# A 7x7 convolution's own steps: another order of reads, scaling and queues

## The chip, the cores and the metric

The kernel runs on one core of a Trainium2 chip. Its time is the device time of one execution in microseconds (us), lower is better. A time of the kernel is the median of several runs; a profiled execution of its own gives the trace.

## The reference

Two residual layers over an input `x` of shape (8, 96, 96, 192) in float32: eight images of 96 x 96 pixels with 192 channels.

```python
# layer 0: group norm, 1x1 projection to 384 channels, 3x3 depthwise convolution,
#          four directional running means, layer norm, 1x1 projection back
x = x + _L0_conv_ref(_gn(x), L0_conv_W_in, L0_conv_b_in, L0_conv_conv_w, ...)
# layer 1
x = x + _L1_conv_ref(_gn(x), L1_conv_dw_kernel, L1_conv_dw_bias, ...)

def _L1_conv_ref(x, dw_kernel, dw_bias, ln_gamma, ln_beta, w0, b0, w1, b1, gamma):
    y = lax.conv_general_dilated(x, dw_kernel, window_strides=(1, 1), padding='SAME',
            dimension_numbers=('NHWC', 'HWIO', 'NHWC'), feature_group_count=c) + dw_bias
    mu = jnp.mean(y, axis=-1, keepdims=True)
    var = jnp.mean(jnp.square(y - mu), axis=-1, keepdims=True)
    y = (y - mu) * lax.rsqrt(var + EPS) * ln_gamma + ln_beta
    y = jnp.einsum('bhwc,cd->bhwd', y, w0) + b0          # 192 -> 768
    y = jax.nn.gelu(y, approximate=False)
    y = jnp.einsum('bhwd,dc->bhwc', y, w1) + b1          # 768 -> 192
    return y * gamma
```

`_gn` is a group norm with 32 groups of 6 channels over a whole image. The depthwise kernel of layer 1 is 7x7, one filter for each channel.

## The kernel before, in words

The kernel has five phases, each with an order of instructions written out by hand (`manual_schedule`): what stands earlier in the code stands earlier in each engine's queue. Phases A to C do layer 0 and leave its result, called x1, in the DRAM tensors `X1_d`, one for each half of the batch (four images). Phase D does the group norm and the 7x7 convolution of layer 1, phase E its layer norm and the two large projections (the "last pass").

**Phase D** runs in steps. `todo` lists 32 of them: for each batch half 16 blocks of 12 channels (two groups of 6). The first `N1` = 19 steps, numbers 0 to 18, run by themselves ("own steps"); the other 13 are fed in small pieces into the first half of phase E. So all of batch half 0 (steps 0 to 15) is convolved before phase E starts. A step n consists of

- `load_raw(n, t)`, t = 0 to 2: x1's rows of the block, each t as two DMAs of 64 partitions (g = 0 and 1). Rows of step n + 2 are loaded during step n, into a buffer that step n's rows leave.
- `load_band(n)`: the convolution's band matrix, one DMA into half of the partitions; a copy on VectorE (`spread` in `scale_steps`) makes the other half.
- `scale_steps(n)`: the group norm as 24 scalings of 128 x 192 elements (8 for each t) from `raw` to `xin`, on VectorE, for steps 1 and 18 (t = 1, 2) and all later ones on ScalarE.
- `conv_d(n, c)`, c = 0 to 5: 12 matmuls into two PSUM banks, and two evictions on ScalarE into `yo` (L1197).
- `store_d(n)`: six DMAs from `yo` to the DRAM tensor `Y_d`, three for each of the block's two groups.

During step n the loop issues, in this order: the first rows of step n + 2, the stores of step n - 1, the rest of the rows and the band of step n + 2, one piece of `norm_c(1)` (the group statistics of batch half 1, from step 3 on), the scalings of step n + 1, and the six convolutions of step n.

DMAs are issued from two engines' queues, SyncE's (SP) and GpSimd's (POOL). The rows of g = 0 and the stores of the first group are SP's, those of g = 1 and of the second group POOL's, and the bands alternate.

**Phase E** works on tiles of `Y_d`. `load_y(n)` reads tile n with 41 pieces: `begin`, which takes the buffers `ya` and `yb`, and 40 DMAs, five for each of eight blocks q of 32 partitions. q = 0 to 5 stand for channel blocks 0 to 5 (each five groups of 6 channels, so that block 0 needs no more than steps 0 to 2, block 4 steps up to 12, block 5 steps up to 14), q = 6 and 7 repeat blocks 4 and 5; the fifth DMA of each q brings a part of the last two groups, which step 15 makes. A tile serves two units u (`per` = 2); there are 72 units. For each unit `norm_steps_e(u)` is the layer norm in seven pieces: `sums`, `mean`, `center` (VectorE), `square` (ScalarE, L1340), `squares`, `powers` (VectorE, and a power on GpSimd, L1352) and `scale` (VectorE). Then `turn_in` transposes on VectorE, `first_layer` projects to 768 channels (L1388, L1398) with a Gelu on ScalarE (L1407), and `second_layer` projects back (L1418), adds the residual `r` (L1429, x1 read by `load_r` and biased by GpSimd, L1269), and stores the output from GpSimd (L1437).

At the end of phase D the two phases overlap: in step 16 (`NI`) the reads of tile 0 are issued between the convolutions, in step 18 those of tile 1; in step 17 the layer norm of unit 0 begins, in step 18 that of unit 1. The scalings of step 18 for t = 1 and 2 are placed on ScalarE three at a time between the evictions of step 17, and the pieces `square` and after it are placed behind its last convolutions:

```python
parts = load_y((n - NI) // 2) if n in (NI, NI + 2) else []
if n >= NI + 1:
    held, chain = chain, norm_steps_e(n - NI - 1)
    for step in chain[:3] + held:
        step()
    chain = chain[3:]
for c in range(GS):
    conv_d(n, c)
    for step in parts[c * 7 : c * 7 + 7]:
        step()
    for step in steps[c * 3 : c * 3 + 3]:
        step()
    if n >= NI + 1 and c >= GS - 3:
        chain.pop(0)()
```

Of the kernel before, what the change touches and what calls it, by code (L numbers as in the profile page):

```python
# [15 lines left out]
GROUPS = 32  # L16
# [85 lines left out]
def conv_blocks_kernel(  # L102
# [716 lines left out]
    def load_raw(n, t):  # L819
# [13 lines left out]
        for g, eng in enumerate((nc.sync, nc.sync if n >= N1 else nc.gpsimd)):  # L833
# [9 lines left out]
    def load_band(n):  # L843
# [5 lines left out]
        (nc.sync, nc.gpsimd)[g and n < N1].dma_start(  # L849
            band[g * 64 : (g + 1) * 64].rearrange("q c l -> q (c l)"),  # L850
            Z2_d[:, i * GC : (i + 1) * GC].rearrange("r c l -> r (c l)"),
        )

    def scale_steps(n):
# [4 lines left out]
        def scale(t, k, b):  # L859
            if (t, k, b) == (0, 0, 0):  # L860
                pool = d_pools[0 if n >= N1 else n % 2]
                xins[n] = pool.tile([128, NT, NH, GC, WV], F32, tag="xin", name="xin")
# [27 lines left out]
    def norm_c(hf, bank):  # L890
# [7 lines left out]
        def means():  # L898
            ms = gp.tile([128, GROUPS], F32, tag="gn_ms", name="gn_ms")
            nc.vector.tensor_reduce(ms, sv[:, :, :, 1], AX.X, ALU.add)  # L900
            t["ps"] = bank()
            nc.tensor.matmul(t["ps"][:, :GROUPS], blk, ms, start=True, stop=True)

        def squares():
            t["gm"] = gm = gp.tile([128, GROUPS], F32, tag="gn_gm", name="gn_gm")
# [12 lines left out]
            ds = gp.tile([128, GROUPS], F32, tag="gn_ds", name="gn_ds")  # L918
            nc.vector.tensor_reduce(ds, d, AX.X, ALU.add)
            t["ps"] = bank()  # L920
            nc.tensor.matmul(t["ps"][:, :GROUPS], blk, ds, start=True, stop=True)

        def powers():
            ve = gp.tile([128, GROUPS], F32, tag="gn_ve", name="gn_ve")
# [21 lines left out]

        def keep():
            nc.vector.tensor_copy(
                s1[:, hf].rearrange("p b a g -> p (b a g)"),
                t["ps"][:, : NH * 2 * GROUPS],  # L950
            )

        return [means, squares, powers, shift, spread, keep]
# [251 lines left out]
    def store_d(n):  # L1205
# [5 lines left out]
        for k, eng in enumerate((nc.sync, nc.sync if n >= N1 else nc.gpsimd)):  # L1211
            y_d = Y_d[hf][:, 2 * i + k].rearrange("r b a n -> r (b a n)")
            eng.dma_start(  # L1213
# [3 lines left out]
            eng.dma_start(y_d[:e], yf[k * 64 : k * 64 + e, 0])  # L1217
            eng.dma_start(y_d[ROWS - e :], yf[k * 64 + KB - e : k * 64 + KB, NB - 1])  # L1218
# [223 lines left out]
    with tc.manual_schedule():  # L1442
        with tc.tile_pool(name="d_own", bufs=1, side="right", **by_tile) as own:
            d_pools[1] = own
            norms, chain = norm_c(1, bank), []
            for n in range(N1):
                if n + 2 < N1:
                    load_raw(n + 2, 0)
                if n:
                    store_d(n - 1)  # L1450
                if n + 2 < N1:
                    for t in range(1, NT):
                        load_raw(n + 2, t)
# [6 lines left out]
                now = len(steps) if n + 2 < N1 else len(steps) // NT  # L1460
# [145 lines left out]
```

## Time and profile before

| | |
|---|---|
| median of 3 runs | 5567.61 us (5566.02 to 5573.98) |
| profiled execution, its own time | 5583.44 us |
| its span, first to last instruction | 5581.6 us |
| PE (matmul) busy | 5300.3 us, 95% |
| DVE, ACT, POOL busy | 65%, 46%, 42% |
| DMA, GpSimd's queue (q0) | 332.38 MB, 18.3% of 16 engines |
| DMA, SyncE's queue (q1) | 673.77 MB, 47.9% of 16 engines |
| convolution, L1187 | 4608 matmuls, 433.2 us busy, 514 ns each |
| evictions, L1197 | 384 on ACT, 198.8 us busy, 579 ns each |
| first layer, L1388 and L1398 | 785.9 and 419.6 us busy |
| second layer, L1418 | 6912 matmuls, 1175.4 us busy |

The profile is of one execution. Engines are PE (TensorE's matmuls), PEld (its weight loads), DVE (VectorE), ACT (ScalarE), POOL (GpSimd) and SP (SyncE). Busy time leaves out issuing and waiting. The idle time ahead of an instruction is put down to what released it; where a wait is for several things, to the one that came last. A share of DMA is the busy share of the core's 16 DMA engines, with both queues together. The mean over the span says little here, since the phases have different limits; the stage of the own steps lies between about 2650 and 3010 us.

### The profile page before, as it was taken

What the parts mean: (1) busy time and instruction counts of PE and PEld (TensorE: products, weight loads), DVE (VectorE), ACT (ScalarE), POOL (GpSimd) and SP (SyncE); (2) the same over time, 40 slices, a digit from 0 to 9 for tenths busy, and PEclk for the clock granted to TensorE, in tenths of its full rate; (3) what the DMA queues carried; (4) which work ended last, traced back from release to release, by engine and by line L of the source; (5) the groups of instructions that cost most, each with busy time, mean ns of one, the idle gap of its engine ahead of it and who ended that gap; (6) DMA issues with size and microseconds to landing.
All of it is one profiled execution on the core that took longest, in us unless ns stands there. A gap on an engine that the chain in (4) does not pass through costs nothing. (4 is left out here: it accounts for less than half of the span.)

```text
span 5581.6 us, 108128 instructions
## 1 busy us (share of the span) xinstructions
PE 5300.3 (95%) x42206; PEld 3355.4 (60%) x42206; DVE 3600.3 (65%) x6722; ACT 2588.8 (46%) x5778; POOL 2320.5 (42%) x2035
## 2 busy tenths in 40 slices
PE   6999989999999999998686999999899999999999
PEld 4666633333333999997343555566566676667667
DVE  6656449999999455555454655555566676776764
ACT  2444447777776556554433444444433233333332
POOL 1111128888887555554222222232233333333332
PEclk9999989999999999999897999999999999999999
DMA  7999879999997899999996554565433332233331
GB/s 221 286 293 264 240 194 243 244 246 241 245 245 205 260 292 287 281 290 275 253 280 157 118 120 108 128 135 135 110 89 92 82 81 77 79 89 90 81 79 40
DMA packets 801788, 1015.29 MB, mean 182 GB/s; under 512 B 331345, under 2 KB 684690, under 8 KB 799229
## 3 DMA queue, kind: packets, MB, share of 16 engines
q1 hardware_dynamic: 713445, 673.77, 47.9%
q0 software_dynamic: 81872, 332.38, 18.3%
q8 instruction: 333, 5.46, 0.4%
q10 hardware_dynamic: 5960, 2.22, 0.2%
q14 instruction: 178, 1.46, 0.1%
HBM read 603.70 MB, written 419.95 MB: 183 GB/s over the span
## 5 line engine op out<-in xcount | busy, mean ns | idle before, releaser
L1418 PEld LDWEIGHTS hp<-w1g,g 128*128 128x128 f32 x6912 | 1118.4, 190 | 141.6 <-issue 73.5
L1418 PE MATMUL hp<-w1g,g 128*128 128x192 f32 x6912 | 1175.4, 329 | 0.0
L1407 ACT ACTIVATE g<-hp,b0g 128x512 f32<-128x512 f32 x864 | 518.3, 690 | 1143.4 <-PE hp L1398 1143.4
L1437 POOL DMA_DIRECT2D out_dram<-xo x288 | 210.6, 731 | 1647.5 <-DVE xo L1429 1561.1
L1388 PE MATMUL hp<-yT,w0w 128*128 128x512 f32 x1728 | 785.9, 601 | 21.8 <-DVE yT L1373 17.6
L1429 DVE TENSOR_TENSOR xo<-hp,r 128x384 f32<-128x384 f32 x288 | 227.5, 790 | 821.6 <-PE hp L1418 812.7
L1026 PE MATMUL po<-wc,mt 128*128 128x193 f32 x3456 | 688.0, 335 | 7.1 <-DVE x1c L1043 6.8
L627 PE MATMUL pl<-pin,band 34*32 34x380 f32 (+1 forms) x13824 | 629.0, 490 | 20.4 <-DMA pin<-P_d 20.4
L701 POOL TENSOR_TENSOR mo<-mo,z 128x768 f32<-128x768 f32 x286 | 597.8, 2090 | 4.4 <-ACT mo L652 0.4
L1026 PEld LDWEIGHTS po<-wc,mt 128*128 128x128 f32 x3456 | 557.6, 192 | 37.8 <-ACT mean L1028 30.4
L1187 PE MATMUL hp<-xin,band 63*64 63x372 f32 (+1 forms) x4608 | 433.2, 514 | 147.0 <-ACT xin L868 50.2
L1388 PEld LDWEIGHTS hp<-yT,w0w 128*128 128x128 f32 x1728 | 324.0, 192 | 387.3 <-issue 349.0
L660 DVE TENSOR_TENSOR_SCAN z<-decay,loc 128x768 f32<-128x768 f32 x288 | 505.5, 1755 | 45.1 <-ACT loc L636 16.7
L669 DVE TENSOR_TENSOR_SCAN z<-decay,z 128x768 f32<-128x768 f32 x288 | 498.3, 1730 | 0.1
L627 PEld LDWEIGHTS pl<-pin,band 34*32 34x32 f32 x13824 | 232.3, 107 | 399.0 <-issue 397.1
L1352 POOL TENSOR_TENSOR rs<-tot,neg_half 32x32 f32<-32x32 f32 x72 | 394.6, 5481 | 94.5 <-DVE tot L1350 94.4
L648 PE MATMUL pa<-loc,mix 128*32 128x384 f32 x3456 | 432.0, 494 | 0.0
L651 PE MATMUL pa<-last,down 96*32 96x384 f32 x1152 | 426.9, 494 | 0.9 <-ACT mo L652 0.9
L1398 PE MATMUL hp<-yT,w0w 64*128 64x512 f32 x1728 | 419.6, 611 | 0.0
L1187 PEld LDWEIGHTS hp<-xin,band 63*64 63x64 f32 x4608 | 212.3, 142 | 337.5 <-issue 187.1
L1197 ACT ACTIVATE yo<-hp,dwb 128x384 f32<-128x384 f32 x384 | 198.8, 579 | 432.2 <-PE hp L1187 308.8
L636 ACT COPY loc<-pl 128x384 f32<-128x384 f32 x576 | 248.1, 483 | 313.1 <-PE pl L627 313.1
(158 smaller groups left out, 7521.6 us busy)
## 6 DMA issues: line engine op xcount, KB each, us to landing
pin<-P_d SPq DMA_DIRECT2D x192, 576.0 KB
P_d<-po POOLq DMA_DIRECT2D x95, 1152.0 KB, 9.7
mt<-M SPq DMA_DIRECT2D x192, 384.0 KB
xq<-in_x_dram SPq DMA_DIRECT2D x96, 576.0 KB
xr<-in_x_dram SPq DMA_DIRECT2D x192, 288.0 KB
X<-x1c SPq DMA_DIRECT2D x144, 384.0 KB
r<-X SPq DMA_DIRECT2D x36, 1536.0 KB
out_dram<-xo POOLq DMA_DIRECT2D x288, 192.0 KB, 2.5
```

What stands on the lines that cost most here:

```text
L627: nc.tensor.matmul(pls[g][at * RB : (at + 1) * RB, :, lo:hi], band[rows, c, kh, :], pin[rows, c, :, NJ - 1 - j, lo + kh - 1 : hi + kh - 1] ...
L648: nc.tensor.matmul(pa[at], mix[:, i, at], loc[:, q], start=True, stop=True)
L651: nc.tensor.matmul(pa[at], down[:, to], last[:, q], start=True, stop=True)
L660: nc.vector.tensor_tensor_scan(zf, decay_f, loc.rearrange("p q n -> p (q n)"), 0.0, ALU.mult, ALU.add)
L669: nc.vector.tensor_tensor_scan(zr, decay_f, zr, 0.0, ALU.mult, ALU.add)
L701: eng.tensor_tensor(m, m, z, ALU.add)
L1026: nc.tensor.matmul(po, lhs[m], wc[:, m], start=(m == 0), stop=(m == NC - 1))
L1187: nc.tensor.matmul(pys[g][k * 64 : (k + 1) * 64, :, lo:hi], band[rows, k * GS + c, d * ZS : d * ZS + 64], xin[rows, :, :, k * GS + c, lo + ...
L1388: nc.tensor.matmul(hps[m, q], w0w[:, 0, m * 128 : (m + 1) * 128], yT[:, 2 * q], start=True, stop=False,)
L1398: nc.tensor.matmul(hps[m, q], w0w[p, 1, m * 128 : (m + 1) * 128], yT[p, 1], start=False, stop=True,)
L1407: nc.scalar.activation(g[:, m, q], hps[m, q], AF.Gelu, bias=b0g[:, m : m + 1], scale=1.0)
L1418: nc.tensor.matmul(po[:, q], g[:, m, q, k * 128 : (k + 1) * 128], w1g[:, m], start=(m == 0), stop=(m == NE - 1),)
```

## The change

Five things change in the own steps.

- Rows: from step 2 to 18 all six row DMAs are issued by GpSimd, ahead of everything else in the step.
- Stores and bands: all are issued by SyncE, in the own steps as later; the band of step n + 2 stands ahead of the stores of step n - 1.
- Tile 0 of the last pass: its reads are issued in steps 12, 13, 14 and 16, as soon as the steps that make their channels have been stored; tile 1's are issued at the end of step 17, ahead of the store of that step.
- The end: in step 17 the band copy and the first three pieces of unit 0's layer norm stand ahead of VectorE's scalings of step 18, and ScalarE's 16 scalings and the `square` stand behind all evictions of step 17. In step 18, unit 0's `squares` and `powers`, unit 1's first three pieces and unit 0's `scale` stand ahead of the convolutions, and unit 1's `square`, `squares` and `powers` behind them.
- `norm_c`: the matmul that sums over partitions is issued with the piece that reads its result, one piece later than before, and `keep` is joined to `spread`.

```diff
@@ load_raw
-        for g, eng in enumerate((nc.sync, nc.sync if n >= N1 else nc.gpsimd)):
+        engs = (nc.sync, nc.gpsimd) if n < 2 else (nc.gpsimd,) * 2 if n < N1 else (nc.sync,) * 2
+        for g, eng in enumerate(engs):
@@ load_band
-        (nc.sync, nc.gpsimd)[g and n < N1].dma_start(
+        nc.sync.dma_start(
@@ norm_c
         def means():
-            ms = gp.tile([128, GROUPS], F32, tag="gn_ms", name="gn_ms")
+            t["in"] = ms = gp.tile([128, GROUPS], F32, tag="gn_ms", name="gn_ms")
             nc.vector.tensor_reduce(ms, sv[:, :, :, 1], AX.X, ALU.add)
+
+        def total():
             t["ps"] = bank()
-            nc.tensor.matmul(t["ps"][:, :GROUPS], blk, ms, start=True, stop=True)
+            nc.tensor.matmul(t["ps"][:, :GROUPS], blk, t["in"], start=True, stop=True)

         def squares():
+            total()
...
-            t["ps"] = bank()
-            nc.tensor.matmul(t["ps"][:, :GROUPS], blk, ds, start=True, stop=True)

         def powers():
+            total()
@@ store_d
-        for k, eng in enumerate((nc.sync, nc.sync if n >= N1 else nc.gpsimd)):
+        for k in range(2):
...
-            eng.dma_start(
+            nc.sync.dma_start(
@@ own steps
-            norms, chain = norm_c(1, bank), []
+            make_xin(1)
+            norms = norm_c(1, bank)
+            y_0, y_1 = load_y(0), load_y(1)
+            early_y = {
+                NI - 4: y_0[:1] + [y_0[1 + q * 5 + b] for q in (0, 1) for b in range(NH)],
+                NI - 3: [y_0[1 + q * 5 + b] for q in (2, 3) for b in range(NH)],
+                NI - 2: [y_0[1 + q * 5 + b] for q in (4, 6) for b in range(NH)],
+                NI: [y_0[1 + q * 5 + b] for q in (5, 7) for b in range(NH)]
+                + [y_0[1 + q * 5 + NH] for q in range(8)],
+                NI + 1: y_1,
+            }
             for n in range(N1):
                 if n + 2 < N1:
-                    load_raw(n + 2, 0)
+                    for t in range(NT):
+                        load_raw(n + 2, t)
+                    if n:
+                        load_band(n + 2)
                 if n:
                     store_d(n - 1)
-                if n + 2 < N1:
-                    for t in range(1, NT):
-                        load_raw(n + 2, t)
+                else:
                     load_band(n + 2)
...
                 steps = scale_steps(n + 1) if n + 1 < N1 else []
-                now = len(steps) if n + 2 < N1 else len(steps) // NT
-                for step in steps[:now] + steps[-1:] * (now < len(steps)):
+                last, on_scalar = [], []
+                if n == NI + 1:
+                    chain = norm_steps_e(0)
+                    per_t = len(steps) // NT
+                    on_scalar = steps[per_t:-1]
+                    steps = steps[-1:] + chain[:3] + steps[:per_t]
+                    on_scalar.insert(per_t, chain[3])
+                    chain = chain[4:]
+                elif n == NI + 2:
+                    nxt = norm_steps_e(1)
+                    steps = chain[:2] + nxt[:3] + chain[2:]
+                    on_scalar = nxt[3:6]
+                    chain = nxt[6:]
+                for step in steps:
                     step()
...
                 for c in range(GS):
                     conv_d(n, c)
-                    for step in parts[c * 7 : c * 7 + 7]:
-                        step()
-                    for step in steps[c * 3 : c * 3 + 3]:
-                        step()
-                    if n >= NI + 1 and c >= GS - 3:
-                        chain.pop(0)()
+                for step in on_scalar + early_y.get(n, []):
+                    step()
```

More of the change, by code (lines that the diff above doesn't have):

```diff
@@ L852, in load_band, with make_xin @@
         )
+    def make_xin(n):
+        pool = d_pools[0 if n >= N1 else n % 2]
+        xins[n] = pool.tile([128, NT, NH, GC, WV], F32, tag="xin", name="xin")
     def scale_steps(n):
@@ L859, in scale @@
         def scale(t, k, b):
-            if (t, k, b) == (0, 0, 0):
-                pool = d_pools[0 if n >= N1 else n % 2]
-                xins[n] = pool.tile([128, NT, NH, GC, WV], F32, tag="xin", name="xin")
+            if n not in xins:
+                make_xin(n)
             c = slice(k * GS, (k + 1) * GS)
@@ L917, in squares @@
             )
-            ds = gp.tile([128, GROUPS], F32, tag="gn_ds", name="gn_ds")
+            t["in"] = ds = gp.tile([128, GROUPS], F32, tag="gn_ds", name="gn_ds")
             nc.vector.tensor_reduce(ds, d, AX.X, ALU.add)
-            t["ps"] = bank()
-            nc.tensor.matmul(t["ps"][:, :GROUPS], blk, ds, start=True, stop=True)
         def powers():
+            total()
             ve = gp.tile([128, GROUPS], F32, tag="gn_ve", name="gn_ve")
@@ L945, in spread @@
                 )
-        def keep():
             nc.vector.tensor_copy(
@@ L951, in keep @@
             )
-        return [means, squares, powers, shift, spread, keep]
+        return [means, squares, powers, shift, spread]
     with ExitStack() as ph:
@@ L1216, in store_d @@
             )
-            eng.dma_start(y_d[:e], yf[k * 64 : k * 64 + e, 0])
-            eng.dma_start(y_d[ROWS - e :], yf[k * 64 + KB - e : k * 64 + KB, NB - 1])
+            nc.sync.dma_start(y_d[:e], yf[k * 64 : k * 64 + e, 0])
+            nc.sync.dma_start(y_d[ROWS - e :], yf[k * 64 + KB - e : k * 64 + KB, NB - 1])
     def place(n):
@@ L1459, in conv_blocks_kernel @@
                 steps = scale_steps(n + 1) if n + 1 < N1 else []
-                now = len(steps) if n + 2 < N1 else len(steps) // NT
-                for step in steps[:now] + steps[-1:] * (now < len(steps)):
-                    step()
-                steps = steps[now:-1]
-                parts = load_y((n - NI) // 2) if n in (NI, NI + 2) else []
-                if n >= NI + 1:
-                    held, chain = chain, norm_steps_e(n - NI - 1)
-                    for step in chain[:3] + held:
-                        step()
-                    chain = chain[3:]
+                last, on_scalar = [], []
[12 more added lines that the diff above has]
+                for step in steps:
+                    step()
                 for c in range(GS):
                     conv_d(n, c)
-                    for step in parts[c * 7 : c * 7 + 7]:
-                        step()
-                    for step in steps[c * 3 : c * 3 + 3]:
-                        step()
-                    if n >= NI + 1 and c >= GS - 3:
-                        chain.pop(0)()
+                for step in on_scalar + early_y.get(n, []):
+                    step()
             store_d(N1 - 1)
```

## The prediction

> **What bounds the kernel now.** I read the page's 40 slices first, to find where PE, which is busy for 95% of the span, has holes.
>
> ```profile
> PE   6999989999999999998686999999899999999999
> DMA  7999879999997899999996554565433332233331
> ```
>
> A slice is 139.5 us. Slices 20 to 22 (2651 to 3070 us) read 6, 8 and 6 for PE, its longest stretch below 9 in the run; here lie the 19 convolution steps. In the first two of them the DMA engines are full, in the third they are not. So it has two limits. The table of stages splits it (times from the span's start, then PE, PEld, DVE, ACT and POOL busy, granted clock, DMA share, GB/s):
>
> ```profile
> core 0: us, PE busy (x) PEld busy (x) DVE busy (x) ACT busy (x) POOL busy (x), PEclk, DMA share, GB/s
> 2684.00:2720.00 36.00, 19.19 (x217) 10.30 (x209) 14.42 (x44) 10.18 (x20) 8.55 (x13) 0.81 1.03 297
> 2720.00:2732.00 12.00, 9.56 (x90) 4.28 (x94) 7.50 (x18) 2.89 (x6) 1.88 (x4) 0.71 0.50 119
> 2732.00:2946.00 214.00, 172.31 (x1872) 98.09 (x1864) 111.17 (x323) 79.24 (x155) 57.43 (x83) 0.91 1.02 282
> 2946.00:3008.00 62.00, 27.16 (x288) 14.53 (x288) 31.89 (x78) 24.18 (x44) 10.60 (x9) 0.74 0.48 116
> 3008.00:3055.00 47.00, 33.50 (x91) 14.64 (x92) 21.71 (x43) 13.62 (x19) 8.71 (x5) 0.76 0.71 160
> ```
>
> Up to 2946 the 16 DMA engines are the limit (share 1.02 to 1.03), but for a hole of 12 us at a share of 0.50. The timeline puts the last eviction (L1197) of step 2 at 2694.5 and that of step 16 at 2945.6: 251.1 / 14 = 17.9 us a step, where neighbouring steps that wait for no data take 11.4. After 2946 neither PE nor DMA is full: there waits decide. The table of waits (total, times, longest) for 2940 to 3060 names them:
>
> ```profile
> DVE s L1325 <- DMA yb<-Y: 39.5, 3, 17.7
> POOL r L1269 <- DMA ya<-Y: 38.3, 1, 38.3
> PE hp L1187 <- ACT xin L868: 27.8, 1, 27.8
> ACT sq L1340 <- DVE ya L1318: 23.1, 1, 23.1
> ```
>
> and the timeline the order (start, duration, engine, line, and in brackets the idle time and who ended it):
>
> ```profile
> 2985.07 1.96 ACT L1340 ACTIVATE sq<-ya 128x1024 f32<-128x1024 f32 x1 [23.11 <-DVE ya L1318]
> 2990.07 13.85 PE L1187 MATMUL hp<-xin,band 63*64 63x384 f32 x144 [27.83 <-ACT xin L868]
> 3008.57 6.32 PE L1388 MATMUL hp<-yT,w0w 128*128 128x512 f32 x8 [4.65 <-DVE yT L1373]
> 3039.68 2.05 PE L1388 MATMUL hp<-yT,w0w 128*128 128x512 f32 x2 [11.78 <-DVE yT L1373]
> ```
>
> Read upwards from PE: step 18 waits 27.8 us for its scaled rows on ACT; ACT stands 23.1 us at the square of the first tile (L1340), placed among the evictions of step 17; the square waits for DVE's centring, and that for the tile's last read from Y. All 41 reads of tile 0 are issued only between 2944.5 and 2978.8. The second tile repeats it: PE stands 11.8 us at 3039.7. From 3100 on PE is 90 to 100% busy, so what is won here reaches the end.
>
> **What the Trainium skill says.** "DMA: Bandwidth & Descriptors", section "Issuing engines are not separate DMA queues": DMAs of all issuing engines run on the same 16 engines and interleave; issuing from several only saves sequencer time. The trace agrees on the sharing: both queues together make up the share of 1.02. Hence moving x1's rows to GpSimd adds no engine. The same page, section "Queues, rings and completion order": each DMA engine goes round robin between the queues it has work for. So splitting rows (one queue) from stores (the other) mixes reads and writes all the time, where before each queue carried a run of stores and then a run of rows. What a mix is worth this trace shows, below. "TensorE: Matmul & The Clock Gate", section "What's actually happening": an idle array falls to half clock. The granted clock of 0.71 to 0.76 in the stretches with holes, against 0.91, agrees; fewer holes give a little more that I don't count.
>
> **The change, part by part.**
>
> *DMA-bound steps.* Rows (L839): 102 issues of 384 KB for steps 2 to 18. Half leave SP for POOL. POOL's issue costs 0.715 us each, 6 a step = 4.3 us; 19 x 3 stores (0.70 + 0.53 + 0.58) and its bands (0.55) leave POOL, so its load is as before and far under a step. POOL's queue loses its 155 us of waits for evictions (L1213), behind which rows stood; rows now wait only for DVE's scaling, which frees their buffers, and for the landing of the row load eight earlier on the queue (so the built program orders it). Behind a waiting row stands one pow of 5.65 us (L928), needed ten steps later: nothing. SP takes 6 stores and one band a step, some 2.5 us of issue; behind its wait for evictions stands only a band for a step later.
>
> The price is DMA time. At equal share the rate differs by what is in flight (windows 2898 to 2903, then 2784 to 2789; q1 is SP's queue, q0 GpSimd's):
>
> ```profile
> DMA packets 675, 1.16 MB, mean 231 GB/s; under 512 B 41, under 2 KB 575, under 8 KB 675
> q1 hardware_dynamic: 664, 1.10, 103.5%
> ```
>
> ```profile
> DMA packets 578, 1.91 MB, mean 383 GB/s; under 512 B 78, under 2 KB 174, under 8 KB 561
> q0 software_dynamic: 298, 1.15, 60.9%
> q1 hardware_dynamic: 280, 0.77, 41.9%
> ```
>
> SP's rows go in packets under 2 KB (575 of 675 here); GpSimd's go in larger ones. Over 2650 to 2946, 79.3 MB move at 268 GB/s: 296 us. Bounds: if only the queue's average counts (q1 39.57 MB in 52.0% of 296 us = 257 GB/s, q0 39.33 MB in 46.0% = 289), 20 MB go over and 19 MB come back, a gain of 0. If the mix is always that of the second window, 79.3 / 0.383 = 207 us, a gain of 89, of which 16 steps at 11.4 us of PE allow no more than about 80. I take 296 GB/s: 6 us from the hole (12 us at half share), which lifts 268 to 274, and a third of the way from there to 340, the middle of two windows rich in GpSimd's packets (297 and 383). 79.3 / 0.296 = 268 us, a gain of 28.
>
> The hole: PE waited 9.6 us for the group sums (L900) and 9.6 us until DVE read the sum out of its bank (L906). The change issues each of these matmuls a step later, just before its reader, so both waits go; in full-DMA time they cost nothing, their worth is the 6 us of the hole, counted above.
>
> *Early reads of tile 0.* 24 of its 40 loads (60 KB each) move into steps 12 to 14, 8 and the 8 small ones to the end of step 16. Each is an SP issue of 0.44 us; 8 in a step are 3.5 us, behind which one band and six stores queue: hidden under 17.9. Their DMA time is not hidden: alone on the queue (2955 to 2978) they make 1.79 MB in 32.2% of 23 us, 240 GB/s; 1.5 MB / 240 = 6 us, lost. Stage: -28 + 6 = **-22 us** (range -70 to +6).
>
> *The tail*, from the start of step 17 (before: 2948.9). DVE: band copy 1.5, sums 1.9 + 1.0, mean 2.7, centring 2.4 = 9.5 us, then 8 scalings, 2.4. ACT: evictions to 12.0; 8 scalings at 0.48 = 3.9; square 2.0 + 1.1, no longer waiting, since centring ends at about 9.5; 8 scalings 3.9: 22.9. PE's step 18 runs 22.9 to 34.3, evictions to 35.1. DVE meanwhile does tile 0's squares and powers and unit 1's sums, mean and centring (both units read tile 0), and pow (5.45 on POOL) lies beside them; scale(0) ends by 34. Then, in order on DVE ahead of the transposes: square of unit 1 on ACT, 3.1 (38.2), squares 1.75 and powers 1.65 (41.6), first transpose 1.0: PE's first L1388 at **42.7**. Before it was 3008.6 - 2948.9 = 59.7: -17. PE's stall of 27.8 becomes one of about 11.5 (17 ACT-side operations now stand ahead of step 18) and the one of 4.7 becomes 8. So "behind evictions" is not free; it is cheaper than the wait.
>
> Then 11.8 us at 3039.7: tile 1's 41 loads, 36 us of issue on SP, now start right after step 16's store, about at 0, and land near 37; first needed after 42.7. -12, with only 6 us of cover: if SP is slower, part returns. Step 17's store and then r's load now stand behind them: issued near 45, landed (15 us as before) and biased (5.4) by 66; first reader L1429 near 74. Tail: **-29 us** (range -42 to -10). The reordered sums of image half 0, in the stage before, are one instruction each: 0 (+-3).
>
> Sum: -22 - 29 = -51. The profiled execution itself took 5583.4 us around a span of 5581.6; the median of the runs is 5567.6. The difference is applied to the median: **5517 us**.
>
> **The rivals.**
> 1. *As above*: 5517, own range 5497 to 5540. Chance 0.50.
> 2. *The DMA engines are full and stay so.* The queue averages (257 against 289, swapped evenly) speak for it; the mixed windows against. Stage +6, or 0 with the hole; tail -26: 5567.6 - 26 + 3 = 5545. Chance 0.20.
> 3. *The mix pays fully*: 340 GB/s, 79.3 / 0.340 = 233, stage -57, tail -29: 5482. For it: 383 and 314 GB/s in windows with stores. Chance 0.15.
> 4. *Tail gives its gain on*: tile 1's reads or r come late and PE stands at 3039's place again: tail -10, stage 0: 5558. Chance 0.04.
> 5. *Slower: x1's rows on one queue become the bound.* Six loads a step, at most eight in flight: a step can't be under 6/8 of a load's landing. The median landing is 13.6 us now (10.2 us a step, harmless), with three rows a step and the stores on that queue. Were it 30 us, a step would take 22.5: 15 x 4.6 = +69, less 29: 5608. It decides from where the 29 are eaten, a step of 17.9 + 29/15 = 19.8 us, a landing of 26.5. Against it: POOL's rows take half of the bytes today within the same landing as stores. Chance 0.11.
>
> **How the numbers follow.** A change under 0.2% (11 us) can't be told from none by a measurement of this kernel. Rivals 1, 2 and 3 are faster: 0.85; rival 4 straddles the limit: same 0.04; rival 5 slower: 0.11. The range leaves out most of rival 5 and the far half of rival 3: 5478 to 5562.
>
> **What would show it.** Right: from step 2 to step 16 a step takes 16 us rather than 17.9; no share of 0.50 near 2725; PE's wait on ACT xin (L868's successor) near 11 us; first L1388 near 43 us after step 17's first matmul; no 11.8 us wait at unit 1. Wrong: DVE's scaling waits longer for raw than 107.6 us in the stage, or POOL's rows land after 20 us and more (rival 5); the rate stays at 268 GB/s (rival 2); sums (L1325) still wait for yb (rival 4).

## The result, and the profile after

The changed kernel takes 5545.5 us, the median of 8 runs (5537.57 to 5560.37), beside 5572.44 us (5564.01 to 5581.5) of the kernel before on the same chip: a ratio of 0.9955, 95% interval 0.9941 to 0.997. So it is faster by 27 us (17 to 33), about half of the 51 us forecast.

Two profiled executions of one kernel differ: the phases before the own steps end anywhere between 2620 and 2652 us in the executions shown here, whatever the kernel. So totals are compared by their medians, and stages by their own length. Three lengths are used throughout, read from the timelines: **own steps**, from the last projection matmul of phase C to step 16's last eviction; **12 to 16**, the part of it between the last evictions of steps 12 and 16; **tail**, from step 16's last eviction to the first Gelu of unit 3.

| kernel | own steps | 12 to 16 | tail |
|---|---|---|---|
| before, first and second profile | 313.0, 300.9 | 67.7, 62.4 | 179.9, 181.8 |
| after, first and second profile | 299.0, 304.7 | 78.0, 76.0 | 156.0, 159.3 |

The own steps have hardly gained, 302 us against 307 in the mean; the tail has, 158 against 181. First the page's 40 slices of the kernel after, as they were read for the kernel before:

```profile
PE   6999989999999999999786999999999999999999
DMA  7999879999997899899996555555433233333331
```

The low stretch is still three slices, 7, 8 and 6 where it was 6, 8 and 6. The table of stages of the kernel after (from and to; busy time of PE, PEld, DVE, ACT and POOL; granted clock, DMA share, GB/s):

```profile
2684.00:2720.00 36.00, 28.98 (x317) 16.97 (x309) 22.14 (x61) 12.26 (x25) 9.96 (x14) 0.91 1.02 327
2720.00:2732.00 12.00, 11.76 (x138) 6.77 (x142) 9.21 (x29) 5.49 (x12) 8.57 (x5) 1.00 1.02 344
2690.00:2860.00 170.00, 148.67 (x1654) 91.43 (x1658) 103.22 (x293) 69.47 (x140) 54.68 (x68) 0.93 1.01 316
2860.00:2935.00 75.00, 50.23 (x557) 35.85 (x552) 27.60 (x76) 23.70 (x48) 8.23 (x13) 0.82 0.88 230
```

Up to 2860 the step has changed as meant: the DMA engines are as full as before, but move 316 GB/s, where the two profiles of before have 274 and 280 in the same stretch (2690 to 2860); the second profile of after has 307. The hole with a share of 0.50 is gone, and a step takes 15.1 us. From 2860 to 2935, in steps 13 to 16, it turns round: 230 GB/s at a share of 0.88, PE busy for only 50 of 75 us, 19.5 us a step. The table of waits from 2640 to 2950 (total, times, longest) shows what is new there:

```profile
POOL raw L840 <- DVE xin L874: 163.5, 40, 24.3
ACT yo L1201 <- DMA Y<-yo: 103.5, 13, 14.9
...
PE hp L1191 <- ACT yo L1201: 69.4, 13, 19.4
...
ACT yo L1201 <- DMA ya<-Y: 27.9, 2, 21.6
```

The last line puts 21.6 us of one eviction's wait (L1201) down to a *read* of tile 0, with which an eviction has nothing to do. What it needs is its output buffer, and so the landing of an older store; but DMAs raise a few semaphores in turn when they land (experiment 2), and the profile takes the wrong one for the releaser. That reads are behind it all the same, the timeline of the kernel after tells (start, duration, engine, line; SPq is SyncE issuing):

```profile
2842.32 14.45 SPq L1250 DMA_DIRECT2D ya<-Y  x8
2856.88 1.33 SPq L850 DMA_DIRECT2D band<-Z_d  x1
2858.32 0.54 SPq L1217 DMA_DIRECT2D Y<-yo  x1
...
2869.33 0.26 SPq L1222 DMA_DIRECT2D Y<-yo  x1
2869.68 15.06 SPq L1250 DMA_DIRECT2D ya<-Y  x8
2884.29 3.88 ACT L1201 ACTIVATE yo<-hp,dwb 128x384 f32<-128x384 f32 x8 [21.61 <-DMA ya<-Y]
2884.86 0.45 SPq L850 DMA_DIRECT2D band<-Z_d  x1
2885.41 0.54 SPq L1217 DMA_DIRECT2D Y<-yo  x1
```

Eight reads take SyncE 14.5 and 15.1 us, not 3.5. Step 12's stores go out from 2858.3 to 2869.3, 8 us and more after its last eviction at 2850.2; step 13's only from 2885.4. There are two output buffers in turn, so step 14's evictions stand until step 12's stores have landed (the last, issued at 2869.3, lands at 2884.1), and PE stands behind them.

The tail, in the timeline of the kernel after (idle time ahead and who ended it in brackets):

```profile
2935.71 1.90 DVE L1329 TENSOR_REDUCE s<-ya 128x32 f32<-128x1024 f32 x1 [11.71 <-DMA yb<-Y]
...
2942.90 1.97 ACT L1344 ACTIVATE sq<-ya 128x1024 f32<-128x1024 f32 x1
2948.75 13.57 PE L1191 MATMUL hp<-xin,band 63*64 63x384 f32 x144 [10.35 <-ACT xin L872]
2970.66 6.51 PE L1392 MATMUL hp<-yT,w0w 128*128 128x512 f32 x8 [8.33 <-DVE yT L1377]
2990.11 3.70 PE L1392 MATMUL hp<-yT,w0w 128*128 128x512 f32 x8
2997.42 0.55 SPq L1267 DMA_DIRECT2D r<-X  x1
3013.56 5.43 POOL L1273 TENSOR_TENSOR r<-r,b1g 128x3072 f32<-128x3072 f32 x1 [38.50 <-DMA ya<-Y]
3019.02 0.79 DVE L1433 TENSOR_TENSOR xo<-hp,r 128x384 f32<-128x384 f32 x1 [23.84 <-DMA ya<-Y]
3032.36 6.77 PE L1422 MATMUL hp<-w1g,g 128*128 128x192 f32 x24 [7.81 <-DVE xo L1433]
```

The square waits for nothing, PE stands 10.4 us ahead of step 18 instead of 27.8 and 8.3 ahead of the first layer, and the 11.8 us ahead of unit 1 are gone. The sums of unit 0 (L1329) do still wait 11.7 us for the last reads of tile 0, which the prediction names as a sign of being wrong. It costs little: the centring of `ya` ends at 2942.5, 0.4 us before ScalarE comes to its square. Then VectorE waits 23.8 us at the first output (L1433) until r is biased at 3019.0 (the brackets name a read here, too, though it is r that is missing). PE's stops that follow, here and 4.1 us at 3019.9, give back 13 us: counted from step 16's last eviction, unit 1's first Gelu comes 36.9 us earlier than in the first profile of before, unit 2's only 23.9.

### The profile page after: what moved, and what is told of

It is laid out like the page before. It is cut to its first block, busy times and chain, and to the rows that moved or that the text cites. A ratio compares the mean times of both kernels' runs of the same rounds, so it can differ in the third digit from the quotient of the medians.

```text
span 5535.8 us, 108053 instructions
## 1 busy us (share of the span) xinstructions
PE 5289.6 (96%) x42206; PEld 3367.3 (61%) x42206; DVE 3595.9 (65%) x6722; ACT 2588.6 (47%) x5778; POOL 2319.7 (42%) x2020
## 2 busy tenths in 40 slices
DMA packets 795469, 1015.27 MB, mean 183 GB/s; under 512 B 330623, under 2 KB 671728, under 8 KB 792912
## 5 line engine op out<-in xcount | busy, mean ns | idle before, releaser
L1392 PE MATMUL hp<-yT,w0w 128*128 128x512 f32 x1728 | 780.9, 598 | 14.9 <-DVE yT L1377 8.3
L1433 DVE TENSOR_TENSOR xo<-hp,r 128x384 f32<-128x384 f32 x288 | 227.4, 790 | 834.4 <-PE hp L1422 810.4
L1392 PEld LDWEIGHTS hp<-yT,w0w 128*128 128x128 f32 x1728 | 321.8, 191 | 377.7 <-issue 339.2
L660 DVE TENSOR_TENSOR_SCAN z<-decay,loc 128x768 f32<-128x768 f32 x288 | 505.5, 1755 | 45.8 <-ACT loc L636 17.3
L1191 PEld LDWEIGHTS hp<-xin,band 63*64 63x64 f32 x4608 | 224.8, 140 | 294.4 <-issue 125.9
L382 PE MATMUL pm<-xT,win 128*128 128x384 f32 x1152 | 392.7, 491 | 0.0
```

Of the source, the lines that this page charges most:

```text
L660: nc.vector.tensor_tensor_scan(zf, decay_f, loc.rearrange("p q n -> p (q n)"), 0.0, ALU.mult, ALU.add)
L1191: nc.tensor.matmul(pys[g][k * 64 : (k + 1) * 64, :, lo:hi], band[rows, k * GS + c, d * ZS : d * ZS + 64], xin[rows, :, :, k * GS + c, lo + ...
L1392: nc.tensor.matmul(hps[m, q], w0w[:, 0, m * 128 : (m + 1) * 128], yT[:, 2 * q], start=True, stop=False,)
```

## Experiments

All lengths are from one profile of each kernel, all ratios against the kernel before from five rounds of runs; "early reads" are the 24 reads of tile 0 in steps 12 to 14. The edits are shown shortened.

**1. What does each part do? (four kernels)** The change once more; the queue part alone on the kernel before; the change without early reads; the change with r's load moved forward.

> The changed kernel once more, with a second profile, beside the others of this set. The pair of profiles at hand differs by 45.8 us of span, the medians of eight runs by 27. If the 45.8 is the luck of two executions, this profile gives a difference nearer 27 and its stretch from step 2's last eviction to step 16's will differ from the first profile's 229 us by several us. If the pair is typical, the ratio here is 0.992 or lower.

The queue part alone takes the kernel before, changes `load_raw`, `load_band`, `store_d` and the order of rows, band and stores as the change does, and leaves reads, scalings and `norm_c`:

> The kernel before with only the queue part: from step 2 on all rows from GpSimd, stores and bands from SyncE, in the changed order. Reads of tiles 0 and 1, scalings, layer norm and the group sums as before. My theory (rows in one queue and stores in the other mix better): steps 2 to 16 at 15 us instead of 17.9, DMA at 315 to 325 GB/s, and with a tail as before some 32 us less than before: ratio 0.994. The rival (the DMA engines were full and stay so; the gain of the change comes from its tail): 17.5 us or more a step, ratio 0.999 to 1.000.

No early reads:

```diff
-    NI - 4: ..., NI - 3: ..., NI - 2: ..., NI: ...,
+    NI: y_0,
     NI + 1: y_1,
```

> The changed kernel, but all 41 reads of tile 0 are issued at the end of step 16, none in steps 12 to 14. My theory: the early reads stop SyncE for 14 to 15 us each time, stores and bands behind them come late, and steps 12 to 16 pay 10 to 17 us for it. So here step 12 to step 16 takes 60 us (15 a step) instead of 78, while the first tile now lands some 36 us after step 16 and step 18 starts about 26 us later: in sum 5 to 12 us slower than the changed kernel. The rival (the early reads are hidden, other things delay steps 12 to 16): step 12 to 16 stays near 78 us, and the sum is 26 us or more slower than the changed kernel.

And r first:

```diff
-            store_d(N1 - 1)
-            load_band(N1)
-            for t in range(NT - 1):
-                load_raw(N1, t)
         gn_pool.close()
...
         load_r(0)
+        store_d(N1 - 1)
+        load_band(N1)
+        for t in range(NT - 1):
+            load_raw(N1, t)
```

> The changed kernel, with the residual's first load ahead of step 18's stores and of step 19's band and rows on SyncE, instead of behind them. My theory: in the changed kernel the second wait of the tail is not gone but moved to the residual, whose first reader stands 23.8 us and PE about 14 us for it; here the residual lands 8 to 13 us earlier and the kernel is 8 to 13 us faster than the changed one (ratio to before about 0.993 to 0.994). The rival (the residual is not on the path, PE has other work): same as the changed kernel within 3 us.

| kernel | median us | ratio, 95% | own steps | 12 to 16 | tail |
|---|---|---|---|---|---|
| the change again | 5546.97 | 0.9952 (0.9936 to 0.9968) | 304.7 | 76.0 | 159.3 |
| queue part alone | 5528.41 | 0.9929 (0.9911 to 0.9947) | 278.4 | 54.4 | 173.2 |
| no early reads | 5537.89 | 0.9939 (0.9923 to 0.9955) | 275.0 | 53.8 | 173.5 |
| r first | 5529.46 | 0.9925 (0.9909 to 0.9941) | 301.9 | 81.3 | 147.1 |

The change's second profile is 36.1 us of span under before's first, not 45.8, so a part of that difference was chance. The queue part alone wins at least as much as the whole change, and as its theory said: 14.7 us a step from 2 to 16. Its two windows, steps 2 to 12 and 12 to 16 (columns as above):

```profile
2690.00:2845.00 155.00, 134.64 (x1523) 77.16 (x1519) 96.23 (x274) 61.38 (x122) 50.07 (x61) 0.94 1.02 321
2845.00:2899.00 54.00, 48.82 (x577) 36.49 (x573) 34.57 (x100) 23.64 (x48) 13.37 (x19) 0.97 0.99 320
```

320 GB/s all the way. It also fills the hole near 2725 (share 1.02 from 2720 to 2732, and PE waits no more than 0.4 us for the group sums), though it leaves `norm_c` as it was. So the early reads take some 25 us from the own steps and give the tail 14 to 17; its theory also said that the kernel without them would be 5 to 12 us slower in sum. Its median is 9 us lower, and the two intervals overlap: that is not borne out. And r was worth 9 to 12 us of the tail, as expected, but it is soon followed by the next two late things, in the timeline of "r first":

```profile
3021.05 0.80 DVE L1433 TENSOR_TENSOR xo<-hp,r 128x384 f32<-128x384 f32 x1 [6.03 <-POOL r L1273]
...
3061.25 1.02 DVE L1329 TENSOR_REDUCE s<-yb 128x16 f32<-128x512 f32 x1 [14.33 <-DMA yb<-Y]
...
3074.58 3.77 PE L1191 MATMUL hp<-xin,band 63*64 63x384 f32 x24 [9.36 <-DVE band L878]
```

VectorE's wait for r falls from 23.8 to 6.0 us, but step 19's band, which r overtook, now stops PE for 9.4.

**2. Why do the early reads cost 25 us? (three kernels)** Their DMA time, counted as 6 us in the forecast; the order in SyncE's queue; or something in the reads themselves. First two ways round SyncE's queue: fewer reads in a step, or another engine.

```diff
-    NI - 4: 8 reads, NI - 3: 8 reads, NI - 2: 8 reads
+    steps 5 to 8 and 11 to 15: 2 to 4 reads each
```

> The change, but tile 0's early reads two to four a step over steps 5 to 8 and 11 to 15 instead of eight in each of steps 12 to 14; the rest at the end of step 16 as in the change. Theory (SyncE's queue): a DMA waits for the landing of the one eight earlier on its queue, so a step can't be shorter than its DMAs on that queue / 8 x their landing: 15 / 8 x about 10.4 us = 19.5 us in steps 12 to 14 of the change. With 9 to 11 a step it is about 13 us, under the 13.6 us that a step takes with no early reads: step 12 to 16 falls from 76-78 us to about 57, the tail stays as in the change; about 5525 us. Rival (the reads' own DMA time): the same bytes are moved in the same full stage, nothing changes: about 5545 us.

With r's load forward as well:

> The spread reads, and r's load issued ahead of step 18's stores and of step 19's band and rows. Theory: both losses are separate, so the sum of both gains: some 20 us in the steps and 10 in the tail, about 5513 us. Rival (the reads' own DMA time is the loss in the steps): only r's part, about 5532 us. Rival (r's wait is given on to step 19's band and rows): as the spread reads alone.

```diff
 def piece(q, b, eng=nc.sync):
...
+    step(nc.scalar)     # the early reads; the others as before
```

> The change, but the 24 early reads of steps 12 to 14 are issued by ScalarE on a queue of its own, at the same place, behind the step's evictions. Bytes, packets and moments stay. Theory (SyncE's queue): SyncE is back to 7 DMAs a step, its stores go out at once; step 12 to 16 falls to about 58 us, less whatever ScalarE's issue of 8 x 0.44 us delays evictions; about 5527 us. Rival (DMA time, or many small packets): nothing changes, step 12 to 16 stays at 76 us, about 5545 us.

| kernel | median us | ratio, 95% | own steps | 12 to 16 | tail |
|---|---|---|---|---|---|
| spread | 5552.34 | 0.9968 (0.9956 to 0.998) | 304.0 | 71.5 | 160.9 |
| spread, r first | 5538.94 | 0.9943 (0.9926 to 0.996) | 294.1 | 67.4 | 152.7 |
| from ScalarE | 5547.58 | 0.9959 (0.9944 to 0.9973) | 298.5 | 72.5 | 159.7 |

All three miss what the theory expected. SyncE's own waits tell why. First those of the change (2840 to 2935):

```profile
SPq L1250 <- DMA Y<-yo: 18.3, 6, 4.9
SPq L1250 <- DMA band<-Z_d: 5.4, 2, 3.2
SPq L1222 <- DMA ya<-Y: 5.2, 2, 3.6
```

Reads (L1250) wait for the landing of stores and of a band, stores (L1222) for that of reads. It is not for their data: in the traces each DMA raises a semaphore when it lands, SyncE's and ScalarE's DMAs take eight such semaphores in turn, GpSimd's eight others, and a read that waits here waits for the semaphore that it will raise itself, that is for the DMA eight earlier. So the second of step 12's reads is issued at 2845.8, when the band that was issued at 2829.5 has landed. From ScalarE (2855 to 2935):

```profile
SPq L1222 <- DMA Y<-yo: 22.7, 3, 8.9
SPq L1221 <- DMA ya<-Y: 14.6, 4, 6.7
```

SyncE's stores (L1221) wait for reads that *ScalarE* issued, and no data passes between the two; the eight semaphores are common to both. So the move to ScalarE did not take the reads off the stores' way, and ScalarE, which was held for 11 us by the first eight reads, kept its own evictions waiting besides. Spread (2738 to 2935):

```profile
SPq L1250 <- DMA band<-Z_d: 26.0, 7, 6.1
SPq L850 <- DMA Y<-yo: 18.9, 7, 5.0
```

With 9 to 11 DMAs in a step the eighth earlier one is still of the same step: reads wait for the band and the stores just issued, and the next band waits in turn. My formula in the expectation (DMAs / 8 x landing) gave 13 us a step and no loss; it averages over a step, and the queue doesn't (a reading of these waits; no run tests it).

**3. The reads' packets, or their number? (three kernels)** The same reads in unbroken stretches:

```diff
-    y[:, chunk * main : (chunk + 1) * main, b, a]                       # 5 x 384 bytes a row
+    y[:, chunk * main + b].rearrange("r b a n -> r (b a n)")[:, :480]   # 1920 bytes a row
```

> The change, but each of the 24 early reads of steps 12 to 14 takes one unbroken stretch of 1920 bytes from each of its 32 rows, where it takes five pieces of 384 bytes; same place in SyncE's queue, same bytes, same step dependences (so tile 0 gets wrong channels). Theory of packets ([...]160 packets of 384 bytes wait for as many packets of rows and bands, and the queue behind the read waits too): with 32 packets a read is issued and done at once; step 12 to 16 falls from 76-78 us to 56-60, the total by some 18 us to about 5527. Rival (a read stands behind stores and the band because the queue takes no more than eight DMAs at a time): the packets don't matter, SyncE still has 15 DMAs in a step, step 12 to 16 stays above 70 us, about 5543 us.

Then four such reads in one DMA, six instead of 24 (the first of the two kernels also issued joined reads for all later tiles, so only its own steps can be read):

> The change, but the 24 early reads of 60 KB are joined into six of 240 KB, two in each of steps 12 to 14, of unbroken stretches of 1920 bytes as in the run before (so tile 0 gets wrong channels). Bytes and packets are those of that run, only the number of DMAs falls. Theory (SyncE's and ScalarE's DMAs share eight places, a DMA waits for the landing of the one eight earlier, and with 15 in a step reads wait for the stores of their own step and the next stores for the reads): with 9 a step the wait is almost gone, step 12 to 16 falls from 75 us to about 58 to 62, the total to about 5525 us. Rival (the reads' bytes or the moment): step 12 to 16 stays at 75 us, the total at 5539 us.

> The six joined reads again (240 KB each, two in each of steps 12 to 14, wrong channels in tile 0), now without the joined reads that the run before also issued for every later tile, which made its total useless. Theory (number of DMAs on SyncE's places): step 12 to 16 67 us as in that run, against 75 with 24 reads of the same bytes and packets; total about 5530 us. Rival: the total is that of the 24 unbroken reads, 5539 us.

| kernel | median us | ratio, 95% | own steps | 12 to 16 | tail |
|---|---|---|---|---|---|
| 24 reads, unbroken | 5539.01 | 0.9945 (0.993 to 0.996) | 294.5 | 75.3 | 156.3 |
| 6 reads, unbroken | 5611.09 | 1.0073 (1.0048 to 1.0098) | 286.6 | 67.5 | 153.5 |
| 6 reads, unbroken, tile 0 alone | 5540.44 | 0.9945 (0.9929 to 0.996) | 281.3 | 64.8 | 153.6 |

With a fifth of the packets, steps 12 to 16 take 75.3 us as they did with all of them, and SyncE is held as long; its timeline in that kernel:

```profile
2841.18 12.74 SPq L1251 DMA_DIRECT2D ya<-Y  x7
...
2862.11 15.07 SPq L1251 DMA_DIRECT2D ya<-Y  x8
```

So packets are not it. With a quarter of the DMAs and the same bytes, 12 to 16 falls by 8 and 10.5 us, in two profiles; two profiles of before differ by 5 in this stretch. The theory expected 58 to 62 us of the first: at 9 a step part of the wait is left, as it was with the spread. The total is the rival's (5540, where the theory said 5530): the medians don't show the gain, and their intervals (16 us wide) are too wide to deny it.

**4. The reads on the queue with room.** GpSimd issues six row DMAs a step, so two more make eight. Blocks 0 to 3 of tile 0, two reads a step in steps 5 to 8 and 11 to 14, the rest at the end of step 16:

```diff
+    for k, (q, b) in enumerate([(q, b) for q in range(4) for b in range(NH)]):
+        early_y[(5 if q < 2 else 7) + k // 2] += [y_0[1 + q * 5 + b]]    # issued by nc.gpsimd
```

> The change, but 16 early reads (blocks 0 to 3) are issued by GpSimd, two a step in steps 5 to 8 and 11 to 14, the other 24 of tile 0 at the end of step 16 on SyncE. GpSimd's DMAs have eight places of their own, and six rows and two reads make eight a step. Theory: no wait for a DMA of the same step comes about on either queue, only the reads' DMA time of about 4 us is left; end of the phase before to step 16 about 282 us, step 12 to 16 about 57; 8 more reads at the end of step 16 cost the tail 3 to 8 us; about 5530 us. Rival (spread reads on SyncE cost all the same, so early reads cost 1 us each wherever they are): about 297 us, no gain, 5545 us or more.

Measured: 5532.62 us, 0.9928 (0.9906 to 0.995); own steps 282.2, 12 to 16 59.0, tail 159.6. This is what the theory said and not the rival's 297. SyncE's waits in it from 2870 to 2933 are these, all of them:

```profile
SPq L850 <- PE hp L1191: 27.2, 4, 7.6
SPq L1221 <- DMA Y<-yo: 16.4, 7, 5.2
SPq L1217 <- ACT yo L1201: 2.0, 4, 0.5
SPq L1222 <- DMA Y<-yo: 1.3, 4, 0.6
SPq L1217 <- DMA Y<-yo: 0.4, 1, 0.4
SPq L850 <- DMA Y<-yo: 0.3, 1, 0.3
```

The band waits for its buffer, stores wait for evictions and for older stores; no read is among them. On GpSimd's queue the theory is only half right, as its own waits show (2740 to 2933):

```profile
POOL raw L840 <- DVE xin L874: 52.8, 20, 11.7
POOL raw L840 <- DMA raw<-X: 27.1, 19, 4.0
```

Rows now wait 19 times for the landing of older rows; in all the own steps of the queue part alone they do so 3 times, for 4.6 us. At eight a step this queue is full as well. But what stands behind there are rows for two steps later, and no store: a wait that costs little. 16 reads cost 4 to 8 us of the own steps (282.2 against 274 to 278 without early reads); 16 x 60 KB at the forecast's 240 GB/s would be 4. By the same measure 24 reads would cost 6 to 12 us, so that of the 25 us the waiting in SyncE's queue is about 13 to 19 (an estimate from these runs).

**5. The other way round: stores off SyncE.** The own steps' stores from ScalarE, reads and bands left on SyncE:

```diff
+        eng = nc.scalar if n < N1 else nc.sync
-            nc.sync.dma_start(y_d...)
+            eng.dma_start(y_d...)
```

> The change, but the stores of the own steps are issued by ScalarE on its own queue; reads, bands stay on SyncE. Then no store stands behind a read, and an eviction waits for its buffer only as long as the store itself takes. Theory of order (the loss is stores, and so evictions, held up behind reads on SyncE): step 12 to 16 falls to about 60 us, about 5530 us, unless ScalarE's issuing of six stores holds up its evictions, which would show as a longer step from 2 to 12 as well (151 us now). Rival (DMA time of small packets): step 12 to 16 stays near 76 us and 2 to 12 at 151; about 5545 us.

Measured: 5559.91 us, 0.9986 (0.9974 to 0.9998); own steps 329.1, 12 to 16 88.7, tail 148.9. It is worse everywhere in the own steps, also from 2 to 12 (167.6 us against 151.0 and 157.0 in the change's two profiles), where there are no reads: the caveat in the expectation. The timeline of this kernel, ScalarE issuing (ACTq):

```profile
2762.20 0.33 ACTq L1218 DMA_DIRECT2D Y<-yo  x1
2770.91 0.27 ACTq L1222 DMA_DIRECT2D Y<-yo  x1
...
2771.66 3.88 ACT L1201 ACTIVATE yo<-hp,dwb 128x384 f32<-128x384 f32 x8 [12.52 <-DMA Y<-yo]
```

Between two stores it stands 8.7 us, with the next step's evictions behind it. This run can't tell the two theories apart; it shows what a store that waits costs on the engine that evicts. Its tail is 7 to 10 us shorter than the change's; why is open.

**6. What is left of the tail (four kernels).** Late reads, but with all scalings of step 18 ahead of unit 0's layer norm, and r first:

```diff
-    steps = steps[-1:] + chain[:3] + steps[:per_t]
-    on_scalar.insert(per_t, chain[3])
+    steps = steps[-1:] + steps[:per_t] + chain[:3]
+    on_scalar.append(chain[3])
```

> The change with no early reads (all 41 of tile 0 at the end of step 16), r's load first, and in step 17 all scalings of step 18 ahead of unit 0's layer norm (on VectorE ahead of the sums, on ScalarE ahead of the square), so that the late reads hold up no convolution. Theory: the steps cost as little as with the queue part alone (about 275 us from the end of the phase before to step 16's last eviction); step 18 starts about 21 us after step 17, and the layer norm of unit 0 is then the chain: reads land at 27, centring to 32, square 35, squares and powers 39, pow 45, scale and transposes, first L1392 near 53 us after step 17's start, against 62 with all reads late and 41 in the change. About 5520 us. Rival (the early reads are needed for the tail's gain): the first layer starts no earlier than with late reads before, only r's 10 us is won: 5528 us.

Then also unit 1's `squares` and `powers` behind unit 0's transposes:

> The kernel with late reads, r's load first and the scalings ahead, in which moreover squares and powers of unit 1 are issued behind unit 0's transposes. Theory: these two stand ahead of the transposes for 4 to 5 us while the first layer waits for nothing else; first L1392 near 49 us after step 16's last eviction instead of 53, about 5526 us. Rival: tile 1's work comes 5 us later and unit 1 gives it back, the same as without: 5530 us.

The same two ideas on the kernel of experiment 4, with r from GpSimd, then with r first on SyncE:

> The same, and r's first load from GpSimd's queue, and squares and powers of unit 1 behind unit 0's transposes. Theory: r no longer stands behind tile 1's reads and the stores on SyncE, 10 us of the tail; the transposes start 4 to 5 us earlier; about 5516 us. Rival (the next late thing, step 19's band and rows or tile 1's reads, eats it): 5528 us.

> 16 early reads from GpSimd two a step, r's first load on SyncE ahead of step 18's stores and step 19's band and rows (on GpSimd it stood ahead of a power and cost 23 us of VectorE's wait), squares and powers of unit 1 behind unit 0's transposes. Theory: the three gains add: own steps 282 us from the end of the phase before, from step 16 to unit 3's first Gelu 159 - 10 - 4 = 145; about 5515 us. Rival (step 19's band and rows, or tile 2's reads, take the place of r): 155 us there, 5525 us.

| kernel | median us | ratio, 95% | own steps | 12 to 16 | tail |
|---|---|---|---|---|---|
| late reads, free scalings, r first | 5530.34 | 0.9922 (0.9907 to 0.9937) | 278.2 | 58.0 | 162.6 |
| ... and late squares | 5524.94 | 0.9918 (0.9904 to 0.9933) | 274.3 | 57.2 | 163.1 |
| GpSimd's two reads, r from GpSimd, late squares | 5526.54 | 0.9919 (0.9899 to 0.9939) | 283.9 | 58.3 | 154.8 |
| ... but r first on SyncE | 5537.09 | 0.9921 (0.9903 to 0.9939) | 280.5 | 57.7 | 149.0 |

Scalings ahead bring the first L1392 from 59.6 us after step 16's last eviction (no early reads) to 53.4, as expected; but the tail falls by 11 us only (173.5 to 162.6), about what r alone was worth, and the total is near the rival's 5528. The late squares bring the first L1392 to 49.2 us, as expected, and unit 3 gives it back (162.6 and 163.1), as the rival said. r from GpSimd's queue put a power behind a load that waits; its timeline:

```profile
2978.07 1.22 POOL L1269 DMA_DIRECT2D r<-X  x1 [33.62 <-DMA Y<-yo]
2979.31 5.45 POOL L1358 TENSOR_TENSOR rs<-tot,neg_half 32x32 f32<-32x32 f32 x1
2984.79 0.38 DVE L1314 COPY m<-rs 32x64 f32<-32x64 f32 x2 [18.37 <-POOL rs L1358]
```

With r first on SyncE the gains add up in the profile (280.5 + 149.0, the smallest sum of all), near the 282 and 145 expected. The total of about 5515 us is missed all the same: two of its six runs lie there (5515.47 and 5516.32), four between 5536 and 5543, and why is open. In the ratios these four and "queue part alone" (0.9929) can't be told apart. The lowest, late reads with late squares, beats both kernels: its interval (0.9904 to 0.9933) lies below both of the change's (0.9941 to 0.997 and 0.9936 to 0.9968).

**7. Before, a second profile.**

> The kernel before once more, for a second profile of it. Theory: the stage's own lengths repeat within some 5 us (313 us from the end of the phase before to step 16's last eviction, 180 us from there to unit 3's first Gelu). Rival: the first profile of before was a slow one in this stage, and a part of the difference between the two profiled executions is only that.

5563.93 us in its one run; own steps 300.9, tail 181.8. The tail repeats within 2 us, the own steps only within 12: the rival. So single profiles of before leave its own steps uncertain by 12 us, and what is said of them above rests on the kernels that were seen to fall together: 294 to 305 with 24 single early reads on SyncE or ScalarE (stores on SyncE), 274 to 284 without.

## Why the prediction was half right

**DMA-bound steps: right in sum, though not in its parts.** Forecast: 268 GB/s becomes 296, -28 us. In the four kernels that have the queue part and no early reads (queue part alone, no early reads, free scalings, late squares) the own steps take 274.3 to 278.4, 30 us under the mean of before (22 to 39 under its two profiles). Over the own steps they move 304 to 309 GB/s, where before has 267 and 276; the forecast's 296 was a little low. From step 2 to 16 a step takes 14.7 us with the queue part alone (forecast 16). But steps 0 to 2, counted from the end of phase C, have grown from 62 to 70 us and more, in the queue part alone too; in the kernel after ScalarE stands 11 us in step 2 for a store of step 0. The forecast said nothing of them. The hole near 2725 is gone, as said, but not for the reason given, the later matmuls of `norm_c`: the queue part alone fills it without them (experiment 1). And one bound doesn't come out of its own figures: 14 or 16 steps times 17.9 - 11.4 us are 91 or 104, not "about 80"; nothing rests on it. The prediction took from the Trainium skill ("DMA: Bandwidth & Descriptors", "Issuing engines are not separate DMA queues") that issuing from another engine adds no engine; the trace agrees, the share stays near 1. But the page expects no more of it than time on the sequencer, and here the two profiles of before moved 273 and 282 GB/s between the last evictions of steps 2 and 12, at a share of 0.99, and the queue part alone 320, at 1.01. Whether larger packets, steadier mixing or the changed order of issue does it, no run here separates.

**Early reads: the step that failed.** "8 in a step are 3.5 us, behind which one band and six stores queue: hidden under 17.9", and only 6 us of DMA time lost. They cost 25: 302 us with them, 276.5 without. The issue was priced as that of a free queue (0.44 us each). With them SyncE has 15 DMAs in a step, a DMA waits until the one eight earlier has landed, and eight reads take 14.5 us. The forecast knew this rule: it used it on GpSimd's queue, where six rows were no danger, and made rival 5 of it; it did not count SyncE's DMAs. SyncE's own waits in the kernel before, from 2695 to 2878, raise the question, and the prediction makes nothing of them:

```profile
SPq L839 <- DMA raw<-X: 34.6, 10, 6.1
...
SPq L1213 <- DMA band<-Z_d: 13.4, 5, 3.3
SPq L1217 <- DMA raw<-X: 13.2, 3, 6.4
```

Stores (L1213, L1217) waiting for the landing of a band or of rows: no data links them, so it is the queue itself that is full, and that with no early read in it.

**The tail: right, and given back in part.** PE's stall ahead of step 18 is 10.4 (forecast about 11.5), ahead of the first layer 8.3 (8). The first L1392 comes 44.0 us after step 17's first matmul (2926.6; forecast 42.7) instead of 59.7: -16, forecast -17. That it fits is in part luck: the sums start 9.1 us into step 17 instead of 1.5, and the centring ends just in time, 0.4 us before ScalarE wants it. Unit 1's 11.8 us are gone. But r was called safe: "issued near 45, landed and biased by 66; first reader near 74". Counted from step 17's start, it was issued at 71 and biased at 92, and the reader stood ready at 69. Again it is SyncE's queue: tile 1's reads began at 19, not at 0, since the last of tile 0's reads and step 16's stores stood before them, and the stores of two steps took another 19 us. So some 10 us came back: -23 in the tail instead of -29.

**The sum.** -5 in the own steps, -23 in the tail, and some -5 from unit 6's first Gelu to the end (2332.0 and 2332.4 us before, 2327.5 and 2326.6 after), which was not forecast and whose cause stays open: -33 by the profiles, at the edge of the interval of the medians, 17 to 33. The -5 in the own steps is less than the 12 us by which before's two profiles differ there.

**The rivals.** Rival 2 named 5545 us, which is what was measured, and even the parts (about 0 in the stage, -26 in the tail) are near; but its mechanism is false, the rate did not stay at 268. It is by luck that the early reads took back what the rate had won. Rival 4 ("tile 1's reads or r come late") is what happened to r, at about half of the 19 us that it named. Rival 5 was wrong of GpSimd (rows land in 12.4 us in the median, 13.6 before), and its mechanism was at work on the other queue.

## What to carry to other kernels

Count the DMAs of each queue in a step, and in a trace the semaphores that they take in turn: that is how many may be under way. From the first one that waits for a landing of its own step, an issue costs a wait for a landing, and everything behind it in the queue waits too. Here that was dear on the queue with the stores, and cheap on the one with rows for two steps later. Before work is put earlier on a queue, read that queue's own waits: in these kernels a wait of a DMA for a transfer with which it shares no data meant that the queue was full. And measure the parts of a change by themselves: here one of them paid for another.

## What the runs showed of the hardware and was not expected

- At nearly the same DMA share the 16 engines moved 274 and 280 GB/s (share 0.98 and 0.99, from 2690 to 2860, two profiles) with rows and stores on both queues, and 307 to 321 (1.01 and 1.02, three profiles) with rows on GpSimd's and stores on SyncE's.
- In this program DMAs issued by ScalarE count against the same eight places (semaphores) as SyncE's: SyncE's stores waited 14.6 us for reads of ScalarE's.
- Cutting the packets of 24 reads of 60 KB from 160 to 32 each changed steps 12 to 16 by no more than 1 to 3 us (75.3 us against 76.0 and 78.0), in a stretch where the queue was held by waits for landings. The two kernels' traces hold 330623 and 326783 packets under 512 bytes, 24 x 160 apart.
